# VectorE joins each half of the accumulated squares as it lands, ahead of the second set of banks

## The chip, the cores and the metric

The kernel runs on one core of one Trainium2 chip. The metric is the device time of one execution in microseconds. Three executions of the kernel before took 1421.2, 1421.21 and 1421.26 us; the median, 1421.21 us, is the time to compare with. The profile is of one further execution, of 1420.45 us, whose span from the first instruction to the last is 1418.7 us. Within the profile all times are counted from the start of that span.

## The reference

The input `x` is 1024 x 512, `weight` is 64 x 512 x 512 (64 embeddings), all in float32. In short:

```python
out_lin     = x @ lin_w.T + lin_b
xv          = einsum('bf,efm->bem', x, weight)
zp          = einsum('bf,efm->bem', square(x), square(weight))
interaction = 0.5 * sum(square(xv) - zp, axis=1)
return out_lin + interaction                        # 1024 x 512
```

The sum over the embeddings of `zp` is one product, `square(x)` by the sum of the squared weights. So the work is 64 products of 1024 x 512 by 512 x 512, whose results are squared and summed, and one more such product for `zp` with a linear layer beside it.

## The kernel before, in words

**Head.** `spin()` (lines 169 to 174) lets VectorE set a tile `zero` to 0 and runs two matmuls of it on TensorE, while the first transfers are under way. Then `lin()` computes the linear layer with 32 matmuls as soon as `lw_sb` (the linear weights) and the pieces of `xs` and `raw_sb` (both hold `x`) land. `lin_out` writes twice the result into two SBUF tensors, `acc0` and `acc1` (`acc[0]`, `acc[1]`), which hold the upper and the lower half of the 1024 rows, index r.

**Middle.** For each of 32 pairs of embeddings the products are computed by a scheme with seven block products in place of eight, on two levels, so 49 small products per pair, with sums and differences of blocks on GpSimd, VectorE and ScalarE. For each pair ScalarE squares the results, and GpSimd issues transfers that add them into `acc0` and `acc1` in place (`squares`, line 378). It likewise collects the squared weights in `w2_sum`, which the profile calls `w_sum`. The last such transfer into `acc0` is that of block `c12`, the last into `acc1` that of `c21`, of the last pair.

**Last stage** (lines 449 to 606). The product for `zp` is done with seven block products at one level, in two passes, s = 0 and s = 1, which the text calls the two sets. Each set covers half of the rows of each half r and has four output blocks b = 2r + u, where u is the half of the columns. A set uses three PSUM banks, `x_last`, `v_last` and `y_last`, on which the seven products are accumulated one after another; a bank is read in between, as its running sum is a result in itself. TensorE's order within a set is 1 (x), 5 (v), 6 (y), 2 (x), 7 (y), 3 (v), 4 (y). Each is eight matmul records in the profile. Of the results, block 0 is read from x after product 2, block 3 from y after 7, block 1 from v after 3, and block 2 from y after 4.

Every output block is `0.5 * acc + bias - 0.5 * (bank)`:
- `last_t(s, r)` (line 535) computes `0.5 * acc[r] + bias` into the tile `t_last` of set s, for both u: two VectorE instructions. It needs all squares of half r. The text calls these instructions joins.
- `scaled` (line 545) lets ScalarE write `-0.5 * bank` into the tile `o_last`.
- `minus_half` (line 552) lets VectorE write `-0.5 * bank + addend` into `o_last`, where the addend is `t_last` or what `o_last` already holds. The text calls it the read of a bank.
- `add_t` (line 565) lets VectorE add `t_last` to `o_last`. It is needed for blocks whose bank was read without `t_last`.
- `store` (line 560) sends one finished block, 256 KB, to HBM from the queue of SyncE.

TensorE's product 4 of a set adds into bank y, so it waits until VectorE has read block 3 from it.

**What sets the order.** The order on each engine is written out by hand: `st.at(t, fn)` puts a piece of work at a nominal time, and `st.run()` emits all pieces sorted by it. The nominal times only sort; each engine works through its own list in that order and waits where an input is missing. `g` is the nominal start of the last stage. Set 0 has its products at g + 0, 3.2, 5.2, 6, 7, 8, 9; set 1 at g + 10, 12, 14, 16, 18, 20, 22 (in TensorE's order as above).

VectorE's list in set 1 before the change is: joins of set 1 from `acc0` and `acc1`; read of block 0; add to block 3; read of block 3; joins of set 0 from `acc0` and `acc1`; adds to the four blocks of set 0; add to block 1; read of block 1; read of block 2. A store follows each finished block.

Of the kernel before, what the change touches and what calls it, by code (L numbers as in the profile page):

```python
# [8 lines left out]
F32 = mybir.dt.float32  # L9
# [19 lines left out]
def kernel(  # L29
# [30 lines left out]
    nc = tc.nc  # L60
    _, _, _, Q = x.shape
    E, F, M = weight.shape
    P = 128
    NK = F // P
    HM = M // 2
    BK = 2 * HM
# [6 lines left out]
    spool = ctx.enter_context(tc.tile_pool(name="spool", bufs=3))  # L73
# [16 lines left out]
    st = Stream()  # L90
# [76 lines left out]
    LIN = {}  # L167

    def spin():
        zero = spool.tile([P, BK], F32, tag="s5", name="zero")  # L170
        nc.vector.memset(zero, 0.0)  # L171
        ps = psum.tile([P, BK], F32, tag="y", name="y_spin", bufs=3)
        for n in range(2):
            nc.tensor.matmul(ps, zero[:, 0:P], zero, start=True, stop=True)  # L174
# [27 lines left out]
    def lin_out(n):  # L202
        nc.scalar.activation(
            rows(n), LIN[n].rearrange("p (u c) -> p u c", u=2), AF.Copy, scale=2.0
        )

    st.at(-40, spin)
    for r in range(2):
        for kk in range(2):
# [239 lines left out]
    g = 49 * NQ  # L449
# [68 lines left out]
    def last_banks(s):  # L518
        for n in "xvy":
            L[n, s] = psum.tile(  # L520
                [P, BK], F32, tag=n, name=f"{n}_last{s}", bufs=2 if n == "x" else 3
            )

        L["o", s] = zpool.tile([P, 2, 2, BK], F32, tag="z", name=f"o_last{s}")
        L["t", s] = zpool.tile([P, 2, 2, BK], F32, tag="z", name=f"t_last{s}")

    def blk(n, s, b):
        return L[n, s][:, b // 2, b % 2]

    def last_p(i, bank, s, start):  # L530
        return lambda: last_product(L[bank, s], i, s, start)

    def last_t(s, r):
        for u in range(2):
            nc.vector.scalar_tensor_tensor(  # L535
                L["t", s][:, r, u].rearrange("p (j c) -> p j c", j=2),
                acc[r][:, 2 * s + u].rearrange("p (j c) -> p j c", j=2),
                0.5,
                bias[:, ts(u, HM)].unsqueeze(1).broadcast_to([P, 2, HM]),
                ALU.mult,  # L540
                ALU.add,
            )

    def scaled(bank, s, b):
        return lambda: nc.scalar.activation(
            blk("o", s, b), L[bank, s], AF.Copy, scale=-0.5
        )

    def minus_half(bank, s, b, addend):
        def fn():  # L550
            a = blk(addend, s, b)
            nc.vector.scalar_tensor_tensor(  # L552
                blk("o", s, b), L[bank, s], -0.5, a, ALU.mult, ALU.add
            )

        return fn

    def store(s, b):
        r, u = b // 2, b % 2
        nc.sync.dma_start(  # L560
            out_dst[r, s, :, u], blk("o", s, b).rearrange("p (j c) -> p j c", j=2)
        )

    def add_t(s, b):
        nc.vector.tensor_add(blk("o", s, b), blk("o", s, b), blk("t", s, b))  # L565
# [8 lines left out]
    for s, ks in ((0, (0, 3.2, 5.2, 6, 7, 8, 9)), (1, (10, 12, 14, 16, 18, 20, 22))):  # L574
        k1, k5, k6, k2, k7, k3, k4 = (g + k for k in ks)
        st.at(k1 - 0.1, lambda s=s: last_banks(s))
        st.at(k1, last_p("1", "x", s, True))
        st.at(k1 + 0.5, lambda s=s: nc.scalar.copy(L["y", s], L["x", s]))
        st.at(k5, last_p("5", "v", s, True))
        st.at(k5 + 0.5, scaled("v", s, 3))  # L580
        st.at(k6, last_p("6", "y", s, False))
        st.at(k6 + 0.5, scaled("y", s, 1))
        st.at(k2, last_p("2", "x", s, False))
        st.at(k7, last_p("7", "y", s, False))
        st.at(k7 + 0.5, minus_half("y", s, 3, "o"))
        st.at(k3, last_p("3", "v", s, False))
        st.at(k3 + 0.5, minus_half("v", s, 1, "o"))
        st.at(k4, last_p("4", "y", s, False))


        if s == 0:
            st.at(k2 + 0.5, scaled("x", s, 0))
            st.at(k4 + 0.5, scaled("y", s, 2))
            continue
        st.at(k2 + 0.5, minus_half("x", s, 0, "t"))
        st.at(k4 + 0.5, minus_half("y", s, 2, "t"))
        for b, k in ((3, k7), (1, k3)):
            st.at(k + 0.4, lambda b=b: add_t(1, b))
        for b, k in ((0, k2), (3, k7), (1, k3), (2, k4)):
            st.at(k + 0.6, lambda b=b: store(1, b))  # L600
    for r in range(2):
        st.at(g + 14.6 + 0.1 * r, lambda r=r: last_t(1, r))
        st.at(g + 18.6 + 0.1 * r, lambda r=r: last_t(0, r))
    for b in range(4):
        st.at(g + 18.8 + 0.02 * b, lambda b=b: add_t(0, b))
        st.at(g + 18.8 + 0.02 * b, lambda b=b: store(0, b))

    with tc.manual_schedule():
        st.run()
# [30 lines left out]
```

## Time and profile before

| part | us | how to read it |
|---|---|---|
| median of three runs | 1421.21 | device time |
| span of the profile | 1418.7 | first to last instruction |
| TensorE (PE) busy | 1409.8 | 99% of the span |
| VectorE (DVE) busy | 919.3 | 65% |
| ScalarE (ACT) busy | 615.9 | 43% |
| GpSimd (POOL) busy | 1169.5 | 82% |
| first matmul starts | 1.46 | spin, after VectorE's memset |
| last group of matmuls starts | 1409.36 | product 4 of set 1 |
| last VectorE instruction ends | 1415.39 | read of block 2 of set 1 |
| store, issue to landing | 2.2 to 2.7 | eight stores of 256 KB |

In the views that list work in order of time, each line has the start in us, the length in us, the engine, the line of the kernel, the operation, the output and inputs by the program's names, and how many instructions were merged. A bracket at the end tells how long the engine stood idle before it, and what ended that. PE is a matmul and PEld a weight load, which overlap. The ends of matmuls are modelled, so the starts are the better guide.

### The profile page before, as it was taken

The numbers are of one execution on the slowest core, as the hardware profiler recorded it, in microseconds if no ns is written. First come the engines' busy times: TensorE is split into PE (matmuls) and PEld (weight loads), VectorE is DVE, ScalarE is ACT, GpSimd is POOL, SyncE is SP. The second block draws the span as 40 slices with busy tenths as digits, with TensorE's granted clock in tenths as the row PEclk, the third lists the DMA queues.
The fourth block names the chain that finished last, engine by engine and source line by source line (L and its number), as shares of the span: only waits on it lengthen the run. The fifth ranks groups of instructions, "written<-read, shape, count | busy, mean of one in ns | idle before, by whom it ended". The sixth has DMA issues, their size and how long they took to land.

```text
span 1418.7 us, 18050 instructions
## 1 busy us (share of the span) xinstructions
PE 1409.8 (99%) x6452; PEld 1226.4 (86%) x6452; DVE 919.3 (65%) x1337; ACT 615.9 (43%) x821; POOL 1169.5 (82%) x1035
## 2 busy tenths in 40 slices
PE   9999999999999999999999999999999999999997
PEld 4888888888888888888888888888888888888886
DVE  7665666665666765666665666666666666566664
ACT  1444444445444445444345444444444444444452
POOL 4688888888988888888888888888888888888883
PEclk9999999999999999999999999999999999999999
DMA  5489889889898889988889988889989888988876
GB/s 185 109 193 215 199 200 203 183 197 213 198 201 199 192 193 206 204 201 200 200 187 197 211 201 200 200 185 194 216 198 202 199 187 190 218 200 199 205 158 149
DMA packets 41289, 276.16 MB, mean 195 GB/s; under 512 B 4464, under 2 KB 7024, under 8 KB 8560
## 3 DMA queue, kind: packets, MB, share of 16 engines
q0 software_dynamic: 27504, 200.29, 69.4%
q1 hardware_dynamic: 12976, 72.62, 17.3%
q10 hardware_dynamic: 720, 2.10, 0.4%
q8 instruction: 52, 0.85, 0.2%
q14 instruction: 37, 0.30, 0.1%
HBM read 72.61 MB, written 2.10 MB: 53 GB/s over the span
## 4 chain that ended last, share of the span: by engine, by line
PE 99%; DVE 1%; DVEq 0%; issue 0%
PE y L284 41%; PE v L284 27%; PE x L284 27%; PE lin L189 2%; PE y_last L506 1%; PE x_last L506 0%; PE v_last L506 0%; PE y_spin L174 0%; DVE o_last L565 0%; DVE t_last L535 0%; DVE o_last L552 0%; DVEq L636 0%; DVE zero L171 0%; DVEq L552 0%
## 5 line engine op out<-in xcount | busy, mean ns | idle before, releaser
L284 PE MATMUL y<-ti,xs 128*128 128x256 f32 x2688 | 653.5, 379 | 0.0
L284 PEld LDWEIGHTS y<-ti,xs 128*128 128x128 f32 x2688 | 510.6, 190 | 69.7 <-issue 0.3
L349 ACT COPY y<-x 128x512 f32<-128x512 f32 x224 | 127.7, 570 | 622.7 <-PE x L284 622.7
L284 PE MATMUL x<-to,xs 128*128 128x256 f32 x1024 | 252.3, 379 | 0.0
L284 PE MATMUL v<-ti,xs 128*128 128x256 f32 x896 | 229.9, 379 | 0.0
L284 PEld LDWEIGHTS x<-to,xs 128*128 128x128 f32 x1024 | 194.6, 190 | 26.5
L258 POOL TENSOR_TENSOR ti<-to 128x512 f32<-128x512 f32 x128 | 181.1, 1414 | 39.9 <-PE y L284 36.6
L244 POOL TENSOR_TENSOR to<-w,to 128x1024 f32<-128x1024 f32 x64 | 158.9, 2483 | 45.6 <-PE v L284 45.6
L373 ACT ACTIVATE z_c<-z_c 128x1024 f32<-128x1024 f32 x192 | 192.6, 1053 | 0.0
L284 PE MATMUL x<-w,xs 128*128 128x256 f32 x768 | 191.9, 379 | 0.0
L284 PEld LDWEIGHTS v<-ti,xs 128*128 128x128 f32 x896 | 170.2, 190 | 23.1
L344 DVE TENSOR_TENSOR z_z<-y,s 128x512 f32<-128x512 f32 x128 | 88.0, 688 | 127.8 <-PE y L284 127.8
L284 PEld LDWEIGHTS x<-w,xs 128*128 128x128 f32 x768 | 145.9, 190 | 20.3 <-issue 0.5
L258 POOL TENSOR_TENSOR ti<-w 128x512 f32<-128x512 f32 x96 | 131.2, 1367 | 31.5 <-PE y L284 19.8
L378 POOL DMA_DIRECT2D acc<-z_c x96 | 84.4, 879 | 57.6 <-ACT z_c L373 47.6
L284 PE MATMUL v<-to,xs 128*128 128x256 f32 x512 | 131.4, 379 | 0.0
L328 DVE TENSOR_TENSOR s<-y,z_z 128x512 f32<-128x512 f32 x160 | 110.4, 690 | 28.7 <-PE y L284 22.8
L390 ACT ACTIVATE w<-w 128x1024 f32<-128x1024 f32 x126 | 126.4, 1054 | 0.0
L344 DVE TENSOR_TENSOR z_c<-y,s 128x512 f32<-128x512 f32 x96 | 66.4, 692 | 89.6 <-PE y L284 89.6
L328 DVE TENSOR_TENSOR s<-v,z_z 128x512 f32<-128x512 f32 x160 | 110.2, 688 | 18.3 <-PE v L284 11.4
L344 DVE TENSOR_TENSOR z_z<-v,s 128x512 f32<-128x512 f32 x128 | 87.7, 685 | 38.3 <-PE v L284 38.3
L284 PEld LDWEIGHTS v<-to,xs 128*128 128x128 f32 x512 | 97.3, 190 | 13.2
(79 smaller groups left out, 1602.4 us busy)
## 6 DMA issues: line engine op xcount, KB each, us to landing
acc<-z_c POOLq DMA_DIRECT2D x96, 1024.0 KB, 7.6
w_sum<-w POOLq DMA_DIRECT2D x63, 1024.0 KB, 7.9
w<-weight SPq DMA_DIRECT2D x62, 1024.0 KB, 6.1
acc<-z_z POOLq DMA_DIRECT2D x32, 1024.0 KB, 8.0
xq<-x SPq DMA_DIRECT2D x2, 1024.0 KB, 5.6
out<-o_last SPq DMA_DIRECT2D x8, 256.0 KB, 2.3
w<-weight ACTq DMA_DIRECT2D x2, 512.0 KB, 8.3
w<-weight SPq DMA_DIRECT2D x2, 512.0 KB, 7.7
```

Source lines behind the costliest of these rows:

```text
L189: nc.tensor.matmul(LIN[n], quarter(r, kk, (0, 1, 3, 2)[2 * s + l])[:, ts(j, P)], lw_sb[:, 2 * kk + l, :], start=(kk == 0 and l == 0), stop ...
L244: nc.gpsimd.tensor_sub(t, a, b)
L258: nc.gpsimd.tensor_sub(t[:, 0:2, :], b[:, :, HM:M], b.rearrange("p l m -> p (l m)")[:, 0:M].rearrange("p (u c) -> p u c", u=2),)
L284: nc.tensor.matmul(ps[:, ts(j, HM)], xsl(i, o)[:, ts(j, P)], rhs, start=(start and j == 0), stop=True, skip_group_check=True,)
L328: nc.vector.tensor_add(o, d[bank], Z[q, addend][:, blk])
L344: nc.vector.tensor_add(Z[q, name][:, blk], d[bank], d[s])
L349: st.at(t0 + 0.5, lambda: nc.scalar.copy(d["y"], d["x"]))
L373: nc.scalar.activation(o, o, AF.Square)
L378: lambda: nc.gpsimd.dma_start(acc[r], Z[q, name], accum_op=ALU.add),
L390: nc.scalar.activation(w2[:, ts(h, 2)], W[q, v][:, ts(h, 2)], AF.Square)
L506: nc.tensor.matmul(ps[:, ts(j, HM)], last_x(i)[:, (0, 1, 3, 2)[2 * s + l], ts(j, P)], last_w(i)[:, l, :], start=(start and j == 0 and l == 0),
```

## The change

The change puts VectorE's list in the last stage into another order, so that the work that depends on the accumulated squares stands ahead of the reads of set 1's banks. Half r = 0 is joined for both sets and added to blocks 0 and 1 of set 0, which are stored at once; then the same for half r = 1 and blocks 2 and 3; then the adds to blocks 3 and 1 of set 1. Only after all these come the four reads of set 1's banks, each followed by its store. Number and kind of the instructions stay the same. The aim is that no work that could have been done earlier stands between the last products and their reads.

VectorE's list after the change is: joins of set 0, then of set 1, from `acc0`; adds to blocks 0 and 1 of set 0; joins of set 0, then of set 1, from `acc1`; adds to blocks 2 and 3 of set 0; adds to blocks 3 and 1 of set 1; reads of blocks 0, 3, 1 and 2 of set 1.

Beside this, `spin()` no longer sets a tile of its own to zero. It reads a constant 0.0, one element per partition, repeated along the row, that the program writes ahead of its start. Its first matmul then waits for nothing on VectorE. Line numbers after the change are smaller by one from there on.

```diff
     def spin():
-        zero = spool.tile([P, BK], F32, tag="s5", name="zero")
-        nc.vector.memset(zero, 0.0)
+        zero = nc.const_aps.tensor(0.0, [P, BK], F32)
         ps = psum.tile([P, BK], F32, tag="y", name="y_spin", bufs=3)
...
         if s == 0:
             st.at(k2 + 0.5, scaled("x", s, 0))
             st.at(k4 + 0.5, scaled("y", s, 2))
-            continue
-        st.at(k2 + 0.5, minus_half("x", s, 0, "t"))
-        st.at(k4 + 0.5, minus_half("y", s, 2, "t"))
-        for b, k in ((3, k7), (1, k3)):
-            st.at(k + 0.4, lambda b=b: add_t(1, b))
-        for b, k in ((0, k2), (3, k7), (1, k3), (2, k4)):
-            st.at(k + 0.6, lambda b=b: store(1, b))
-    for r in range(2):
-        st.at(g + 14.6 + 0.1 * r, lambda r=r: last_t(1, r))
-        st.at(g + 18.6 + 0.1 * r, lambda r=r: last_t(0, r))
-    for b in range(4):
-        st.at(g + 18.8 + 0.02 * b, lambda b=b: add_t(0, b))
-        st.at(g + 18.8 + 0.02 * b, lambda b=b: store(0, b))
+        else:
+            st.at(k2 + 0.5, minus_half("x", s, 0, "t"))
+            st.at(k4 + 0.5, minus_half("y", s, 2, "t"))
+            for b, k in ((0, k2), (3, k7), (1, k3), (2, k4)):
+                st.at(k + 0.6, lambda b=b: store(1, b))
+    for r, t in ((0, 11), (1, 13)):
+        st.at(g + t, lambda r=r: last_t(0, r))
+        st.at(g + t + 0.1, lambda r=r: last_t(1, r))
+        for u in range(2):
+            st.at(g + t + 0.2, lambda b=2 * r + u: add_t(0, b))
+            st.at(g + t + 0.2, lambda b=2 * r + u: store(0, b))
+    for b in (3, 1):
+        st.at(g + 15, lambda b=b: add_t(1, b))
```

## The prediction

> **What bounds the kernel now.** I read the busy totals first, then the chain of waits, then the order of work in time over the last 25 us and the first 15, since the diff touches only those two ends.
>
> The totals and the chain, from the page:
>
> ```profile
> PE 1409.8 (99%) x6452; PEld 1226.4 (86%) x6452; DVE 919.3 (65%) x1337; ACT 615.9 (43%) x821; POOL 1169.5 (82%) x1035
> ...
> PE 99%; DVE 1%; DVEq 0%; issue 0%
> ```
>
> TensorE is busy for 1409.8 of 1418.7 us and carries 99% of the chain. Only what is on the chain outside TensorE can be won: the first 1.46 us, and everything after the last product. The order in time at the end of the program shows the second:
>
> ```profile
> 1405.91 1.89 PE L506 MATMUL y_last<-tw,sx 128*128 128x256 f32 x8
> ...
> 1407.64 1.89 PE L506 MATMUL v_last<-w_sum,sx 128*128 128x256 f32 x8
> 1407.89 0.69 DVE L552 SCALAR_TENSOR_TENSOR o_last<-y_last,o_last 128x512 f32<-128x512 f32 x1 [0.44 <-PE y_last L506]
> 1408.50 2.49 DVE L535 SCALAR_TENSOR_TENSOR t_last<-acc,bias 128x512 f32<-128x512 f32 x4
> 1409.15 1.70 PEld L506 LDWEIGHTS y_last<-tw,xq 128*128 128x128 f32 x8
> 1409.36 1.89 PE L506 MATMUL y_last<-tw,xq 128*128 128x256 f32 x8
> 1410.90 3.09 DVE L565 TENSOR_TENSOR o_last<-o_last,t_last 128x512 f32<-128x512 f32 x5
> 1414.10 0.69 DVE L552 SCALAR_TENSOR_TENSOR o_last<-v_last,o_last 128x512 f32<-128x512 f32 x1
> 1414.71 0.68 DVE L552 SCALAR_TENSOR_TENSOR o_last<-y_last,t_last 128x512 f32<-128x512 f32 x1
> ```
>
> Columns: start, length, engine, line. The y group of eight records that starts at 1405.91 is read by VectorE at 1407.89, so a bank can be read 1.98 us after its group starts. The v group of 1407.64 is then readable at 1409.62 and the last y group of 1409.36 at 1411.34. VectorE reaches them at 1414.10 and 1414.71: it is working through nine instructions, four joins (L535) and five adds (L565), one every 0.60 us (2.49 us for four; 3.09 for five). The last bank lies ready for 1414.71 - 1411.34 = **3.37 us**. From the end of the last read, 1415.39, to the end of the span, 1418.7, the last store takes 3.3 us more.
>
> The same view earlier shows where VectorE had time to spare:
>
> ```profile
> 1394.42 1.17 POOL L378 DMA_DIRECT2D acc<-z_c  x1
> ...
> 1398.08 1.28 DVE L535 SCALAR_TENSOR_TENSOR t_last<-acc,bias 128x512 f32<-128x512 f32 x2
> ...
> 1402.77 1.29 DVE L535 SCALAR_TENSOR_TENSOR t_last<-acc,bias 128x512 f32<-128x512 f32 x2 [3.40 <-DMA acc<-z_c]
> ...
> 1406.17 0.69 DVE L552 SCALAR_TENSOR_TENSOR o_last<-x_last,t_last 128x512 f32<-128x512 f32 x1 [2.10 <-issue]
> ```
>
> `acc0` is usable at 1398.08 at the latest. `acc1` lands at about 1402.77: its last accumulating transfer is issued at 1394.42. VectorE idles 3.40 us before that landing and 2.10 us after its first join.
>
> At the head:
>
> ```profile
> 1.46 3.78 PE L174 MATMUL y_spin<-zero 128*128 128x512 f32 x4 [1.46 <-DVE zero L171]
> ...
> 8.93 0.42 DVE L157 TENSOR_TENSOR xs<-raw_sb,xs 128x256 f32<-128x256 f32 x1 [7.52 <-DMA xs<-x]
> 8.93 0.30 PEld L189 LDWEIGHTS lin<-lw_sb,xs 128*128 128x128 f32 x2 [0.61 <-issue]
> ```
>
> TensorE starts only when VectorE's memset has ended. But at 8.93 a weight load starts late (0.61 us idle where its neighbours have 0.24) at the very moment at which VectorE is released by the transfer of `xs`. Both read that transfer. TensorE's pace is set by it there, not by its start.
>
> **What the Trainium skill says.**
> - "TensorE: Matmul & The Clock Gate", section on the array's architectural detail: VectorE works strictly first in, first out, while TensorE may pull weight loads ahead of running matmuls. The trace agrees: weights at 1409.15 for matmuls at 1409.36, and VectorE stands for 3.40 us on `acc1` with nothing passing it. So order on VectorE is everything here.
> - The same page, Part 1: the array runs at half clock until a free-running window of about 3.4 us was busy. The trace agrees on the halves: the spin's records start 0.86 us apart, records after 6.4 us 0.43 us apart.
> - "VectorE: DVE Perf Modes", "The DRAIN you can't avoid": a semaphore between two VectorE instructions costs nothing extra. Agrees: the adds wait for earlier VectorE work and still follow at 0.60 us.
> - "DMA: Bandwidth & Descriptors", "Anatomy of one DMA": about 2.0 us fixed, most of it the receipt of the write. The trace has 2.2 to 2.7 us from issue to landing for each 256 KB store.
>
> **The change part by part.**
> 1. The zero tile and its memset (0.48 us of VectorE, start 0.92) go; the two spin matmuls read a constant written before the start barrier (GpSimd, 0.25) with step zero, and wait for nothing. TensorE starts at about 0.9 in place of 1.46, 0.55 us earlier. Its four spin records then end at about 4.5, its first weight load is tied to `lw_sb`, seen landed by 4.31, so `lin` also starts some 0.5 us earlier and TensorE arrives at the `xs` wait at about 8.45. That transfer's issue (SyncE) is untouched, so it still waits until 8.93. Worth: **0**. Ends: 0.55 gained if the transfer comes earlier too; 0.2 lost if the first matmul behind a wait starts a weight load's length (0.19) after it rather than at 8.98.
> 2. No VectorE instruction of the last stage is added or removed: eight joins, six adds, six reads of banks stand in another order. After the first set's last read (1397.48), VectorE now does two joins of set 0 and two of set 1 from `acc0`, then two adds: six at 0.60 from 1398.08, done by about 1401.8. Nothing needed by TensorE is behind them there; they fill the idle stretch. Cost 0.
> 3. Then it waits for `acc1` as before, until L = 1402.77, and does four joins, two adds of set 0, two adds of set 1: eight at 0.60, to L + 4.82 = 1407.59. Behind these stand all four reads of set 1's banks. Block 0 (x) is ready since 1406.17 and is read at 1407.59, 1.4 us later than now; nothing overwrites that bank. Block 3 (y) is read from 1408.19 to 1408.88, 0.3 us later than now. TensorE's last y group adds into this bank and waits for that read: it starts at 1409.36, so **0.48 us of slack** remain. Cost 0, but this is the tight place.
> 4. After that VectorE is ahead of TensorE: v is read when ready at 1409.62, the last y at 1411.34. The nine instructions (5.4 us) that stood between them are gone; of these 3.37 us lay on the path. Gain **3.37**.
> 5. Stores. Now six of the eight (1.57 MB) are issued after 1411.5; the engines move 343 GB/s from about 1412.5 to 1417.3, 0.76 us per store, while stores come every 0.60. The last one therefore queues a little. Afterwards it is alone: v's store is issued 1.7 us ahead. Between the best and the worst landing lie 0.5 us; I take 0.1, ends 0 and 0.4. The two early stores are issued near 1401.2 and 1401.8. A store's bytes begin to move about 0.95 us after its block is done (the first add of the burst ends at 1411.58, bytes from 1412.5), so at 1402.1; `acc1`'s bytes fall from 164 GB/s in 1401 to 1402 to 16 in 1402 to 1403. They hardly meet. Cost 0; upper end: both stores served first, 0.52 MB / 343 GB/s = 1.5 us on L.
>
> Sum: 3.37 + 0.1 = 3.5 us. The span ends near 1415.2, and 1421.21 - 3.5 = **1417.7 us** (0.25% less).
>
> **The rivals.**
> - *The early stores delay `acc1`.* L becomes 1404.3; block 3's read ends 1.5 us later and uses up the slack, so TensorE's last group slips by 1.5 - 0.48 = 1.0 us. Gain 2.5: 1418.7, which is within 0.2%. For it: the 0.48 us, and both use the same engines. Against: `acc1` is nearly done by then.
> - *The head counts too.* If the transfer of `xs` is not what paces TensorE, the 0.55 us come on top: 1417.2. Against: the common release at 8.93.
> - *A new wait takes the place of the old, and the kernel is slower.* VectorE stands on `acc1` with four reads behind it, and TensorE's last group stands behind one of them. With L late by d the end moves by d - 0.48. To lose more than 0.2% (2.84 us), d must exceed 3.5 + 2.84 + 0.48 = 6.8, a landing 15.2 us after its issue; the three accumulates there took 7.0 to 8.5. Were it doubled from 8.35 to 16.7, L would be 1411.1, d 8.35, and the time 1417.7 + 7.9 = 1425.6. Against: GpSimd's order and issue are untouched.
>
> **How the numbers follow.** Forecast 0.80; late `acc1` 0.10; head as well 0.06; slower 0.04. The forecast's own ends (item 5 and the 0.2 of item 1) are 1417.4 and 1418.0; reaching to the late-`acc1` case and the head case gives 1417.2 to 1418.7, leaving under 1 in 10 out. Faster by over 0.2% means below 1418.37: 0.80 + 0.06 = 0.86. Same 0.10, slower 0.04.
>
> **What would show it.** Right: eight instructions of joins and adds back to back on VectorE directly after the landing at about 1402.8; the last two bank reads released by TensorE, with idle time before them, at about 1409.6 and 1411.3; about 3.3 us from the last read's end to the end of the span; TensorE's weight load at about 8.9 still released with `xs`. Wrong: a gap in TensorE ahead of its last group (the slack of 0.48 was less), a landing of `acc1` after 1403.3, a spin that starts at 0.9 with `lin` ending earlier too (the head counted), or a last store that takes as long as before plus a queue.

## The result, and the profile after

| | executions | median us | lowest to highest |
|---|---|---|---|
| before | 6 | 1421.08 | 1420.13 to 1421.26 |
| after | 6 | 1416.72 | 1416.2 to 1419.02 |

The ratio is 0.9972, with a 95% interval of 0.996 to 0.9985: 4.36 us less. The direction is the one forecast, but the time lies below the range, which ended at 1417.2 us. Two comparisons with more executions give 1416.95 and 1416.67 us for the same kernel, against 1420.88 and 1420.76 us for the kernel before, so 3.9 to 4.1 us. One of the six executions took 1419.02 us, 2 us more than the others; no profile caught it, and its cause is open.

The totals and the chain of the page of after:

```profile
PE 1409.5 (100%) x6452; PEld 1226.0 (87%) x6452; DVE 918.2 (65%) x1336; ACT 615.8 (44%) x821; POOL 1169.3 (83%) x1035
...
PE 99%; DMA 0%; SPq 0%; DVE 0%; issue 0%
```

TensorE's work is the same. Of VectorE only the bank read (line 551) is left in the chain, at under half a per cent, and a transfer has come into it, that of `xs`, which belongs to the head. The end of the program in order of time, kernel after:

```profile
1402.18 2.50 DVE L534 SCALAR_TENSOR_TENSOR t_last<-acc,bias 128x512 f32<-128x512 f32 x4 [1.06 <-DMA acc<-z_c]
...
1404.60 2.49 DVE L564 TENSOR_TENSOR o_last<-o_last,t_last 128x512 f32<-128x512 f32 x4
...
1407.01 0.68 DVE L551 SCALAR_TENSOR_TENSOR o_last<-x_last,t_last 128x512 f32<-128x512 f32 x1
1407.61 0.68 DVE L551 SCALAR_TENSOR_TENSOR o_last<-y_last,o_last 128x512 f32<-128x512 f32 x1
1408.50 1.70 PEld L505 LDWEIGHTS y_last<-tw,xq 128*128 128x128 f32 x8
1408.71 1.89 PE L505 MATMUL y_last<-tw,xq 128*128 128x256 f32 x8
1408.91 0.69 DVE L551 SCALAR_TENSOR_TENSOR o_last<-v_last,o_last 128x512 f32<-128x512 f32 x1 [0.63 <-PE v_last L505]
1410.64 0.69 DVE L551 SCALAR_TENSOR_TENSOR o_last<-y_last,t_last 128x512 f32<-128x512 f32 x1 [1.03 <-PE y_last L505]
```

Eight instructions follow the landing of `acc1` back to back, and then the four reads. The last two reads now have idle time ahead of them that TensorE ends: VectorE now waits for the products, where before the finished products waited for VectorE. Block 3's read ends at 1408.29, 0.42 us before TensorE's last group starts. From the start of TensorE's last group to the end of the span it was 1418.7 - 1409.36 = 9.34 us and is 1414.4 - 1408.71 = 5.69 us: the last stage is 3.65 us shorter.

But that last group itself also starts 0.65 us earlier than before. Where this comes from shows at the head. TensorE's second and third group of `lin`, kernel before:

```profile
7.27 1.88 PE L189 MATMUL lin<-lw_sb,raw_sb 128*128 128x512 f32 x4
8.98 3.22 PE L189 MATMUL lin<-lw_sb,xs 128*128 128x512 f32 x7
```

The head, kernel after:

```profile
0.78 3.48 PE L173 MATMUL y_spin<-const-float32-0.0 128*128 128x512 f32 x4 [0.78 <-PEq L628]
...
6.15 1.88 PE L188 MATMUL lin<-lw_sb,raw_sb 128*128 128x512 f32 x4
...
8.28 0.42 DVE L157 TENSOR_TENSOR xs<-raw_sb,xs 128x256 f32<-128x256 f32 x1 [8.28 <-DMA xs<-x]
8.28 0.30 PEld L188 LDWEIGHTS lin<-lw_sb,xs 128*128 128x128 f32 x2 [1.08 <-issue]
8.31 4.10 PE L188 MATMUL lin<-lw_sb,xs 128*128 128x512 f32 x9 [0.28 <-DMA xs<-x]
```

`xs` releases VectorE at 8.28 in place of 8.93, and TensorE starts the third group of `lin` (the first matmuls that need this transfer) at 8.31 in place of 8.98. The groups of `lin` are four records each, 0.43 us apart at full pace, so TensorE was ready for the third at 7.27 + 4 x 0.43 = 8.99 before, and would have been ready at 6.15 + 4 x 0.43 = 7.87 after. So before, it did not wait for `xs` (landed at 8.93) at all: it came to the third group just as the transfer was there. After, it waits 0.4 us. The question for the experiments was which of the two, the earlier spin or the earlier landing, gave these 0.67 us.

### The profile page after: what moved, and what is told of

It reads as the page before. It is cut to its first block, busy times and chain, and to the rows that moved or that the text cites. A ratio compares the mean times of both kernels' runs of the same rounds, so it can differ in the third digit from the quotient of the medians.

```text
span 1414.4 us, 18051 instructions
## 1 busy us (share of the span) xinstructions
PE 1409.5 (100%) x6452; PEld 1226.0 (87%) x6452; DVE 918.2 (65%) x1336; ACT 615.8 (44%) x821; POOL 1169.3 (83%) x1035
## 4 chain that ended last, share of the span: by engine, by line
PE 99%; DMA 0%; SPq 0%; DVE 0%; issue 0%
PE y L283 41%; PE v L283 27%; PE x L283 27%; PE lin L188 2%; PE y_last L505 1%; PE v_last L505 0%; PE x_last L505 0%; DMA xs<-x 0%; SPq L113 0%; DVE o_last L551 0%
```

## The experiments

"Before" in each table is the kernel before, run between the others on the same chip. The three comparisons ran on three chips; the medians of before agree within 0.12 us, so differences across tables are uncertain by about that much.

### First: one part at a time

`tail_only` is the changed kernel with the memset put back; `spin_only` is the kernel before with the memset taken out. The edit of `tail_only` (that of `spin_only` is its reverse):

```diff
-        zero = nc.const_aps.tensor(0.0, [P, BK], F32)
+        zero = spool.tile([P, BK], F32, tag="s5", name="zero")
+        nc.vector.memset(zero, 0.0)
```

> Only VectorE's new order in the last stage; the spin keeps its memset. Theory 1 (both parts count: TensorE's own late start at 1.46 set the pace of the head before, and the transfer of xs landed no later than that): 3.4 to 3.7 us faster than before, so about 0.6 us slower than the whole change; lin's third group of matmuls starts near 8.98 again. Theory 2 (only the new order counts, and xs merely landed earlier by chance in the profile of after): as fast as the whole change within 0.2 us. Theory 3 (the memset and the wait for it made the transfers of x slower): as theory 1 in time, but xs lands near 8.9 here and near 8.3 wherever the memset is gone.

> Only the spin without its memset; the last stage in its old order. Theory 1: 0.3 to 0.8 us faster than before (up to the 1.1 us by which TensorE is ready earlier, cut off by the landing of xs). Theory 2: no difference over 0.2 us. Theory 3: 0.6 us faster, with xs landing near 8.3.

`after_again` has no edit.

> The changed kernel again, unaltered, beside the others. About 4.3 us faster than before on theories 1 and 3, 3.6 on theory 2 if the first profile was a lucky one. Its profile gives a second landing of xs for a spin without memset: 8.2 to 9.0 on theories 1 and 2, near 8.3 on theory 3.

`spin3` is the changed kernel with a longer spin:

```diff
-        for n in range(2):
+        for n in range(3):
             nc.tensor.matmul(ps, zero[:, 0:P], zero, start=True, stop=True)
```

> The changed kernel with three spin matmuls in place of two, so that TensorE comes to the xs wait 0.5 to 0.9 us later, without a memset. Theory 1: loses 0.2 to 0.6 us against the whole change, as TensorE's own arrival sets the start again. Theory 2: same as the whole change. Theory 3: xs lands near 8.3 and TensorE's arrival, about 8.7, sets the start: loses about 0.4 us.

| kernel | executions | median us | ratio to before (interval) |
|---|---|---|---|
| before | 27 | 1420.88 | |
| tail_only | 9 | 1417.19 | 0.9975 (0.9965 to 0.9985) |
| spin_only | 13 | 1420.69 | 0.9999 (0.9991 to 1.0007) |
| after_again | 8 | 1416.95 | 0.9973 (0.9962 to 0.9983) |
| spin3 | 8 | 1417.31 | 0.9975 (0.9965 to 0.9985) |

The new order alone gives 3.7 us. The spin alone gives 0.2 us, which its interval doesn't tell from nothing. The profile of `after_again`, at the head, shows why the 0.67 us of the first profile can't be put down to the spin:

```profile
4.33 3.02 PE L188 MATMUL lin<-lw_sb,xs 128*128 128x512 f32 x4
7.18 1.88 PE L188 MATMUL lin<-lw_sb,raw_sb 128*128 128x512 f32 x4
9.87 0.43 DVE L157 TENSOR_TENSOR xs<-raw_sb,xs 128x256 f32<-128x256 f32 x1 [9.87 <-DMA xs<-x]
9.91 0.67 PE L188 MATMUL lin<-lw_sb,xs 128*128 128x512 f32 x1 [0.85 <-DMA xs<-x]
```

It is the same program as after, and here `xs` lands at 9.87, 1.6 us later. That refutes theory 3, in which the missing memset brings the landing to 8.3, and theory 1's fixed 0.6 us. Theory 2 is right in that the landing varies from execution to execution; whether the earlier spin adds a little is taken up below. `spin3` shows the other case, in which TensorE itself is late:

```profile
8.38 0.43 DVE L157 TENSOR_TENSOR xs<-raw_sb,xs 128x256 f32<-128x256 f32 x1 [8.38 <-DMA xs<-x]
...
9.41 0.59 PE L188 MATMUL lin<-lw_sb,xs 128*128 128x512 f32 x1
```

`xs` is there at 8.38, and the third group starts only at 9.41, when TensorE has worked off the two groups ahead of it. In time `spin3` is not told from `after_again`: its median is 0.36 us higher, its mean 0.16.

### Second: the slack, the stores, and two attempts at a better version

`tail_plus2` is the changed kernel with two joins, those of set 1 from `acc1`, done twice:

```diff
+    st.at(g + 14, lambda: last_t(1, 1))
     for b in (3, 1):
         st.at(g + 15, lambda b=b: add_t(1, b))
```

> The changed kernel with the two joins of set 1 from acc1 done twice (the same values again), so that VectorE reaches the four reads two instructions, 1.2 us, later. If TensorE's last group has the 0.42 us of slack that the profile of after shows (block 3's read ends at 1408.29, the group starts at 1408.71), the slack is used up and the end moves by 1.2 - 0.4 = 0.8 us, with a gap of that length in TensorE ahead of its last group: 9.34 - 5.72 = 3.6 us of gain in the last stage become 2.8. Rival (the reads that stand behind the joins cost nothing, the last one alone counts): no change over 0.2 us and no gap in TensorE.

`stores_late` leaves VectorE's order alone and issues set 0's four stores late, between the last two stores of set 1:

```diff
-            st.at(g + t + 0.2, lambda b=2 * r + u: store(0, b))
+            st.at(g + 20.65, lambda b=2 * r + u: store(0, b))
```

> The changed kernel with the same order on VectorE, but the four stores of set 0 issued late, between the last two stores of set 1, so that all bytes meet at the end as they did before the change. If the time of the stores' bytes (0.76 us each at 343 GB/s) matters as much as VectorE's order: five stores ahead of the last one begin to move near 1410.6 and the end comes about 2 us later than in the changed kernel. Rival (only VectorE's order matters; the spread of the stores gave the 0.24 us by which the last store's landing is shorter than before): at most 0.3 us later.

`late_w` moves two of the first weight transfers from ScalarE's queue to SyncE's, behind those of `x`:

```diff
-            for kk, queue in enumerate((nc.scalar, nc.sync)):
+            for kk, queue in enumerate((nc.sync, nc.sync)):
```

> The changed kernel with the first pair's weights all issued from SyncE's queue behind the transfers of x, so that less traffic competes with xs. If lin's third group starts at the later of two times, TensorE's own readiness (7.9 to 8.9) and the landing of xs (8.3 to 9.9 over six profiles), and competing traffic sets the second: xs lands by about 8.2, 0.3 to 0.8 us faster than the changed kernel, and less spread from run to run. Rival (xs's landing is set by its own fixed latency and size): the same time within 0.2 us. Third: the later weights hold up GpSimd's first differences and so TensorE near 33 us, slower by up to 3 us.

`split_last` is `late_w` with the last read and store in halves:

```diff
-            st.at(k4 + 0.5, minus_half("y", s, 2, "t"))
-            for b, k in ((0, k2), (3, k7), (1, k3), (2, k4)):
+            for j in range(2):
+                st.at(k4 + 0.5, lambda j=j: last_half(j))
+            for b, k in ((0, k2), (3, k7), (1, k3)):
                 st.at(k + 0.6, lambda b=b: store(1, b))
...
+    def last_half(j):
+        o = blk("o", 1, 2)[:, ts(j, HM)]
+        nc.vector.scalar_tensor_tensor(
+            o, L["y", 1][:, ts(j, HM)], -0.5, blk("t", 1, 2)[:, ts(j, HM)],
+            ALU.mult, ALU.add,
+        )
+        queue = (nc.sync, nc.scalar)[j]
+        queue.dma_start(out_dst[1, 1, :, 0, j], o)
```

> late_w with the last bank read in two halves of 256 columns, each stored by a transfer of 128 KB of its own, from SyncE's and ScalarE's queues. Two reads of about 0.42 us in place of one of 0.69, and 0.38 us of bytes after the last in place of 0.76: the end 0.2 to 0.4 us earlier than in late_w. Rival (a store's landing is a fixed time whatever its size): no gain, or 0.1 us slower.

| kernel | executions | median us | ratio to before (interval) |
|---|---|---|---|
| before | 37 | 1420.77 | |
| tail_plus2 | 15 | 1418.04 | 0.9982 (0.9974 to 0.9989) |
| stores_late | 13 | 1419.16 | 0.9989 (0.9981 to 0.9997) |
| late_w | 12 | 1417.16 | 0.9976 (0.9968 to 0.9985) |
| split_last | 8 | 1417.18 | 0.9974 (0.9964 to 0.9984) |

**The slack is real.** The end of `tail_plus2` in order of time:

```profile
1410.27 0.68 DVE L551 SCALAR_TENSOR_TENSOR o_last<-y_last,o_last 128x512 f32<-128x512 f32 x1
...
1411.00 1.59 PEld L505 LDWEIGHTS y_last<-tw,xq 128*128 128x128 f32 x8 [1.24 <-DVE o_last L551]
1411.00 1.99 PE L505 MATMUL y_last<-tw,xq 128*128 128x256 f32 x8 [0.84 <-DVE o_last L551]
```

Block 3's read ends at 1410.95, and TensorE, idle for 0.84 us, starts its last group 0.05 us later. The two joins and their waits cost VectorE 1.4 us, not 1.2 (from the landing of `acc1`, at 1403.45 here, to this read it is 6.82 us against 5.43); less the slack of 0.42 that leaves 1.0, and the median is 1.1 us above `after_again`'s. The forecast for this run was 0.8. So in the changed kernel TensorE's chain is less than one VectorE instruction away from waiting: the slack of 0.42 us is shorter than the 0.60 us at which the joins and adds follow one another.

**The early stores matter as well.** With VectorE's order unchanged, issuing them this late costs 1419.16 - 1416.95 = 2.2 us, more than half of the gain. Work in each stretch of `stores_late`; after the stretch and its length come the busy times and counts of PE, PEld, VectorE, ScalarE and GpSimd, then the granted clock, the busy share of the DMA engines, and what the transfers moved, in GB/s. The last line is the issue of the last store, from the order in time:

```profile
1412.00:1413.00 1.00, 0.00 (x0) 0.00 (x0) 0.65 (x1) 0.00 (x0) 0.00 (x0) 1.00 1.03 335
1413.00:1414.00 1.00, 0.00 (x0) 0.00 (x0) 0.00 (x0) 0.00 (x0) 0.00 (x0) 1.00 1.03 347
1414.00:1415.00 1.00, 0.00 (x0) 0.00 (x0) 0.00 (x0) 0.00 (x0) 0.00 (x0) 1.00 1.04 338
1415.00:1416.00 1.00, 0.00 (x0) 0.00 (x0) 0.00 (x0) 0.00 (x0) 0.00 (x0) 1.00 1.03 345
...
1413.76 0.66 SPq L559 DMA_DIRECT2D out<-o_last  x1
```

VectorE is done at 1412.65, and the transfers then go on at 335 to 347 GB/s, as in the busiest stretches at the end of the kernel before (339 to 347). The loss has two halves. SyncE is still issuing the four late stores, and so issues the last one only at 1413.76, 1.1 us after its block is done; in after it is 0.03 us (1411.33 to 1411.36). And the last store's bytes stand behind those of the others: it lands 3.2 to 3.3 us after its issue in place of 2.2. Only this one late place was run, so the 2.2 us are the price of this place and not of every order in which the stores could leave.

**No better version.** In `late_w` `xs` lands at 9.10, and in `split_last`, with the same head, at 9.32: within the spread of the others, so nothing shows that competing traffic from these weights sets it, and the median is that of the changed kernel within the noise. Two of the twelve executions of `late_w` took 1419.39 and 1419.77 us; whether the later weights held up TensorE in them, the third case of the expectation, is open, as the profile is of another execution. In `split_last` the halves land 1.7 and 1.8 us after issue in place of 2.2, but the second is issued at 1412.48, after two reads that take longer together (0.76 us) than one; its landing comes 4.5 us after the start of TensorE's last group, against 4.8 in after, yet the span ends 5.8 us after it (after: 5.7). What lengthens the closing stretch there is open.

### Third: the spin's share

`tail_only_b` and `after_b` repeat `tail_only` and the changed kernel; `no_spin` takes the spin out of the changed kernel:

```diff
-    st.at(-40, spin)
```

> The new order with the memset kept, a second time, for the share of the spin: its runs and those of the first time against the changed kernel's. If the spin without memset is worth something: again 0.2 us or more slower than the changed kernel beside it. If the 0.24 us of the first time were chance: the order of the two turns round or the gap closes. The last stage, from the start of TensorE's last group to the end, takes 5.7 us either way.

> The changed kernel a third time, beside tail_only_b: 1416.7 to 1417.2 us. Its profile gives one more pair of times for the rule that lin's third group starts at the later of TensorE's readiness and the landing of xs; the last group then starts 1400.4 us after it.

> The changed kernel without any spin, so that TensorE starts cold when the linear weights land, at about 4.33. Rule of the later of two times: lin's first eight records run at half pace, 0.86 us each[...], so TensorE is ready for the third group at 9.5 to 11.2, later than xs lands; 0.5 to 1.5 us slower than the changed kernel. Rival (the landing of xs sets the start in any case): the same time within 0.2 us.

| kernel | executions | median us | ratio to before (interval) |
|---|---|---|---|
| before | 29 | 1420.76 | |
| tail_only_b | 9 | 1417.06 | 0.9975 (0.9965 to 0.9985) |
| after_b | 8 | 1416.67 | 0.9973 (0.9963 to 0.9983) |
| no_spin | 18 | 1417.82 | 0.998 (0.9973 to 0.9987) |

The medians of `tail_only` and the changed kernel differ by 0.24 us in the first comparison and by 0.39 us here. Over both together the new order with the memset has a median of 1417.09 us (18 executions) and the changed kernel 1416.95 us (16): 0.14 us, with single executions spread over 1.4 to 2 us. The means differ by 0.21 us, and drawing the executions anew many times gives an interval of -0.2 to 0.6 us. The starting of the spin 0.7 us sooner is worth little, and not told from nothing. The spin itself is worth more: without it TensorE is ready at 9.43, although `xs` landed at 7.50, and the kernel is 1.15 us slower than `after_b`. The expectation of 9.5 to 11.2 was a little too late: four records of `lin` ran at half pace (7.71 - 4.13 = 3.58 us), the next four at full pace (9.43 - 7.71 = 1.72 us).

The profiles show how the head works. Eight of the thirteen; "ready" is the start of `lin`'s second group plus 4 x 0.43 us; "landed" is VectorE's release by `xs`:

| profile | TensorE ready | xs landed | third group starts | last group starts | difference |
|---|---|---|---|---|---|
| before | 8.99 | 8.93 | 8.98 | 1409.36 | 1400.38 |
| after | 7.87 | 8.28 | 8.31 | 1408.71 | 1400.40 |
| tail_only | 8.43 | 9.23 | 9.26 | 1409.66 | 1400.40 |
| after_again | 8.90 | 9.87 | 9.91 | 1410.31 | 1400.40 |
| spin3 | 9.42 | 8.38 | 9.41 | 1409.74 | 1400.33 |
| tail_only_b | 8.11 | 8.65 | 8.69 | 1409.10 | 1400.41 |
| after_b | 8.13 | 7.99 | 8.12 | 1408.45 | 1400.33 |
| no_spin | 9.43 | 7.50 | 9.43 | 1409.77 | 1400.34 |

The third group starts at the later of the two times, and TensorE's last group follows 1400.3 to 1400.4 us behind it. This holds in the other five profiles too, with one exception, which confirms the slack: in `tail_plus2` it is 1411.00 - 9.60 = 1401.40 us, the 1.0 us by which TensorE waits there. The landing of `xs` lies anywhere from 7.5 to 9.9 over all thirteen, in the changed kernel alone from 8.0 to 9.9. What moves it is open; the earliest landing is that of `no_spin`, and one profile can't tell whether that is chance.

## Why the prediction was right or wrong, point by point

- **What put the time below the range.** The main mechanism, the 3.37 us of part 4, was right. The step of the reasoning that failed is part 1, the head at "Worth: 0"; but it does not carry the miss alone. Three terms add up, and the largest is the base: the forecast took 3.5 us off 1421.21, the median of three executions, while the 93 executions of the kernel before in the three comparisons have a median of 1420.8. So of the 0.75 us between the forecast of 1417.7 and the 1416.95 us of `after_again`, about 0.4 are the base, 0.14 the last stage (9.34 - 5.73 = 3.61 against 3.47, where 5.73 is the mean of the eight profiles with the new order and its stores unaltered, 5.69 to 5.76), and the rest, 0.2, the head with its chance. Counted from 1420.8, the range would have been 1416.8 to 1418.3, and of the three medians of the changed kernel, 1416.72, 1416.95 and 1416.67, one lies in it.
- **Part 1, the head at 0: the step that failed.** It took the landing of `xs` at 8.93 for a fixed time that the change can't move ("so it still waits until 8.93"), and read from one late weight load that TensorE was waiting for it. But the landing is a chance time, of which the prediction had one profile, and in that profile TensorE's own readiness, 8.99, tied with it: its matmuls ran up to 8.98 at their pace, so the late weight load had cost nothing. In the profile of after the landing came early, and TensorE, ready sooner, could use it: 0.67 us of its 4.3 us shorter span. This is the prediction's own sign for being wrong, a spin that starts earlier with `lin` earlier too. In the medians the part is worth 0.14 us over both comparisons, between 0.2 and 0.4 in each by itself, and not told from nothing; the range's lower end allowed for 0.5 in total.
- **How much sooner TensorE is ready** was put at 0.55 us. In after it was 1.1 us, as `lin` ran at full pace almost from its first record; in `after_again`, with the same code, it was 0.1 us, as the first records ran at half pace. Four records of `lin` took 6.15 - 4.33 = 1.82 us in one execution and 7.18 - 4.33 = 2.85 us in another. This agrees with what the Trainium skill says in "TensorE: Matmul & The Clock Gate", Part 1: the window is free-running, so how many matmuls of one kernel run slow differs from run to run.
- **Part 2, VectorE's idle stretch takes the joins of `acc0`: right.** No TensorE instruction waits for them.
- **Part 3, eight instructions after the landing: right.** Block 0 is read 4.83 us after it (forecast 4.82), the slack was 0.42 us (forecast 0.48), and TensorE does not wait; `tail_plus2` shows that it would.
- **Part 4, 3.37 us: right, and 0.05 short.** VectorE, waiting, reads the last bank 1.93 us after its group starts, not 1.98: 1410.64 - 1408.71 against 1414.71 - 1409.36 is 3.42 us.
- **Part 5, the stores at 0.1 us: right kind, too small.** From the end of the last read to the end of the span it is 3.07 us against 3.31, so 0.24; the range of 0 to 0.4 held it. What was not seen is how much can hang on the stores: with the four of set 0 held back to the end, 2.2 us are lost again. That the early stores hardly disturb `acc1` was right: it lands 8.43 us after its issue in place of 8.35. The early stores themselves suffer: the two issued before `acc1` has landed take 2.7 and 4.0 us to land.
- **The rivals.** A late `acc1` did not come. "The head counts too" came nearest, 1417.2, but not as it was meant: the landing does pace TensorE in most profiles (nine of thirteen), and the earlier start helps only where the landing is early. The slower case had its mechanism, VectorE's order holding up TensorE, seen only in `tail_plus2`.

## What to carry to other kernels

When an engine works strictly in order, put what waits only for early inputs ahead of what reads the last products, and then check the other side: which engine waits for a read that now stands later, and by how much. Look at its stores too: held back to the end, they delay the last one twice, in being issued and in moving its bytes. Don't take a transfer's landing at the start of a program for a constant from one profile, and a median of three executions for the base of a forecast of a few tenths of a per cent.

## What the runs showed of the hardware that was not expected

The landing of one 256 KB transfer at the start varied by 1.9 us between three executions of one program (7.99 to 9.87) and by 2.4 us over the thirteen profiles (7.50 to 9.87), while the first piece of the linear weights released TensorE's first weight load of `lin` between 3.97 and 4.49. TensorE also came to its full pace at different times in executions of one program, with `lin`'s first four records taking from 1.82 to 2.85 us. And four transfers that wait in front of another on SyncE's queue cost it twice in `stores_late`: its issue comes 1.1 us after its data are ready, and its landing takes 3.2 to 3.3 us in place of 2.2.
